# Order of x's load and h's transfers, place of h's transposes and sums, and slots of the second-level weight factors in a two-layer graph kernel

## The chip, the cores and the metric

The kernel runs on one core of a Trainium2 chip. The core has five engines with a program of their own each: TensorE (PE, matrix products), VectorE (DVE), ScalarE (ACT), GpSimd (POOL) and SyncE (SP, which here only starts transfers). The metric is device time in microseconds (us) of the whole program, median of several runs.

## What is computed

`x` is 64 x 256 x 512 in float32, `adj` a 256 x 256 matrix of zeros and ones. Cut to what matters:

```python
h = jnp.maximum(_layernorm(x, axis=-1), 0.0)
q, k, v = h @ Wq.T, h @ Wk.T, h @ Wv.T            # per batch, D = 512
rel = adjacency.T[None] * jnp.einsum('bnd,bmd->bnm', q, k)
rel = rel / jnp.linalg.norm(rel, axis=2, keepdims=True)
x = x + jnp.einsum('bnm,bmd->bnd', rel, v)        # layer 0
h = jnp.maximum(_layernorm(x, axis=-1), 0.0)
x = x + jnp.einsum('nm,bmd->bnd', adj, h) @ weight + bias   # layer 1
```

## The kernel before

**Tiles.** Batches go in 32 pairs of two. The x of a pair is a tile of 128 x 4 x 512 in one of five places of a ring (`x_ring`): pair i + 4 is loaded into the place that pair i - 1 leaves when its result has been stored. Wq and Wk are folded into one matrix M before the loop, so that the scores are h M h. Every large product is done by Strassen-Winograd's scheme with seven block products; the products with M (g), Wv (v) and the last weight (mix) take it a second level down for one part of the blocks. Such a scheme needs sums and differences of blocks made beforehand on DVE: `left_factors` (lines 173 to 176) for the moving side, `right_operands` (lines 135 to 138) for the other.

**Stages of one step.** `steady(i)` runs for i = 1 to 28 and works on five pairs at once: it applies the scores of pair i (`attend_and_v`, products of line 662, takes of line 669), makes the scores of pair i + 1 (`scores`, line 311), makes g and v of pair i + 2 (`g_and_v`, lines 287, 299, 478 and 525), turns h of pair i + 3, multiplies pair i by adj (`gather_steps`, line 739, copied out by ACT at line 743) and by the last weight (`mix_and_v`, lines 299 and 525, takes of lines 773 and 534). The first and last pairs have functions of their own.

**What sets the order.** PE, DVE and ACT run under a hand-written order: each stage is a list of products, and a dictionary says which small pieces of work are written down behind the product of that number ("slots"). An engine keeps that order: an instruction that waits holds up all that is behind it on its engine. SP and POOL are not in the hand-written order; their instructions follow a scheduler's order. On SP's queue, one step starts sixteen transfers of h (line 440), one load of x (line 90) and sixteen transfers of rel (line 586); POOL adds the bias in four instructions (line 723) and starts the store (line 794).

**h turned.** The normalised h of pair i + 3 must be transposed. Sixteen transfers move its 32 x 32 squares to their mirrored places (`place_blocks`, into the one tile `blocks`), and eight DVE instructions (`transpose_blocks`, line 450) turn each square. Then come the four sums of the left factors (lines 173 to 176, 128 x 512 each). The tile `blocks` is a scratch of ACT's row sums (lines 358 and 364) as well.

**v's differences.** `attend_operands` gives four steps `v_steps` (lines 135 to 138, into `v_room`, `v` and the two halves of `placed`), one for each of Winograd's right factors; the last is used by the last product of `attend_and_v` alone.

**A bank and its take.** A product goes to a bank of PSUM, and is then taken: the first into a block is copied by ACT (line 464 for g, 513 for v), the later ones are added by DVE (line 466 for g, 515 for v, 487 and 534 at the second level). A product that starts anew in `bank_a` has to wait for the take before it. In `g_and_v` the order of products is a1, c5, a6 with g1, v's a1, a7 with g2, v's c5, a4 with g3, numbered 0 to 6 for the slots.

Of the kernel before, what the change touches and what calls it, by code (L numbers as in the profile page):

```python
# [19 lines left out]
def kernel(  # L20
# [256 lines left out]
    def run_steps(steps, side):  # L277
        for at, step in enumerate(steps):
            step()
            run(side.get(at, ()))  # L280
# [153 lines left out]
    def place_blocks(i):  # L434

        h = H.pop(i)
        hv = h.rearrange("p c (d e) -> p c d e", e=P)
        for j in range(P // S):
            for k in range(P // S):
                nc.sync.dma_start(  # L440
                    out=blocks[ts(j, S), :, :, ts(k, S)], in_=hv[ts(k, S), :, :, ts(j, S)]
                )
# [275 lines left out]
    def add_bias(i):  # L718

        xt = flat(X[i])  # L720
        add = nc.gpsimd.tensor_tensor
        return [
            (lambda c=c: add(xt[:, c, :], xt[:, c, :], bias_bc, ALU.add)) for c in range(TC)  # L723
        ]
# [167 lines left out]
    w_right, w_steps = weight_operands(w_sb, "w")  # L892
    m_second, m_second_steps = second_right(m_right, "m2")
    wv_second, wv_second_steps = second_right(wv_right, "wv2")
    w_second, w_second_steps = second_right(w_right, "w2")
# [34 lines left out]
    def first_pairs(exact):  # L930


        sums = transposes_by_matmul(0)
        stats, root, end, relus = ln0(1)
        run(sums)
        project_g(0, {
            0: stats[0:1] + [lambda: load(3, nc.scalar)],
            1: stats[1:2] + [lambda: load(4, nc.scalar)],
            2: stats[2:4] + [root, load_w_and_bias], 3: [end] + relus,
            4: wv_steps[0:2], 5: wv_steps[2:3], 6: wv_steps[3:4],  # L940
        })
        place_blocks(1)
        turned1, sums1 = transpose_blocks(1)
        gs = g_operands(0)
        stats, root, end, relus = ln0(2)
        project_v(0, {
            0: gs[0:2], 1: gs[2:3] + stats[0:1], 2: gs[3:4] + stats[1:2], 3: stats[2:3],
            4: stats[3:4] + [root], 5: [end], 6: turned1[0:2],
        })
        masks, squares, norm_root, inverse, scales, place, turns = scores(0, {  # L950
            0: turned1[2:4], 1: turned1[4:6], 2: turned1[6:8], 3: relus[0:1] + sums1[0:1],
            4: relus[1:2] + sums1[1:2], 5: relus[2:3], 6: relus[3:4],
        })
        place_blocks(2)
        stats, root, end, relus = ln0(3)
        project_g(1, {
            0: sums1[2:4] + masks[0:1], 1: masks[1:2] + squares[0:2] + stats[0:1],
            2: squares[2:4] + stats[1:2], 3: [norm_root] + stats[2:3],
            4: [inverse] + scales + [place] + stats[3:4] + [root], 5: [end] + w_steps[0:1],
            6: w_steps[1:4],  # L960
        })
        gs = g_operands(1)
        turned2, sums2 = transpose_blocks(2)
        project_v(1, {
            0: gs[0:2], 1: gs[2:3] + turned2[0:2], 2: gs[3:4] + turned2[2:4] + relus[0:2],
            3: turned2[4:6] + relus[2:4] + w_second_steps[0:4],
            4: turned2[6:8] + m_second_steps[0:4],
            5: m_second_steps[4:8] + turns[0:2], 6: turns[2:4],
        })
        place_blocks(3)  # L970
        masks, squares, norm_root, inverse, scales, place, turns = scores(1, {
            0: sums2[0:1], 1: sums2[1:2], 2: sums2[2:3], 3: sums2[3:4], 5: w_second_steps[4:8],
        })
        stats, *parts = ln1(0, exact)
        h_second = second_h.pop(2)()
        attend(0, by_slot({c: [stats[c]] for c in range(TC)}, {
            0: masks[0:1], 1: masks[1:2] + squares[0:2], 2: squares[2:4] + [norm_root],
        }))
        turned3, sums3 = transpose_blocks(3)
        if exact:  # L980
            nc.vector.tensor_copy(adjt_r, adjt_sb)
        g, v = g_and_v(2, by_slot(layer_1(parts), {
            1: h_second + [inverse], 2: turned3[0:4], 3: scales + [place] + turned3[4:8],
            4: add_bias(0) + wv_second_steps[0:4], 5: sums3[0:2], 6: wv_second_steps[4:8],
        }))
        v_steps, rel_steps = attend_operands(1)
        y_products, y_steps = gather_steps(0, exact)
        run_steps(y_products, {
            0: sums3[2:3], 1: sums3[3:4], 2: y_steps[0:1], 3: v_steps[0:1],
        })  # L990
        y_second = second_of_y(0)
        totals, mean, row_squares, *norm0 = norm_by_scalar(flat(X[4]))
        run(y_steps[1:2])
        mixed = mix_and_v(0, g, v, {
            0: y_steps[2:4] + totals[0:2], 1: y_second[0:4] + totals[2:4],
            2: y_second[4:8] + [mean] + row_squares[0:2], 3: v_steps[1:2] + row_squares[2:4],
            4: turns + rel_steps[0:2] + norm0[0:2], 5: rel_steps[2:4] + v_steps[2:4],
        })
        return norm0[2], mixed, v

    def steady(i, exact, relu0, mixed, v):

        gs = g_operands(i + 1)
        relus0 = relus_of_h(i + 3, relu0)
        stats, root, end, relus, uppers, lowers = ln1(i, exact)
        halves = [stats[b * NC + t] for t in range(NC) for b in range(NB)]
        attend_and_v(i, mixed, v, {  # L1010
            0: relus0[0:2], 1: relus0[2:4] + gs[0:1], 2: gs[1:2],
            3: gs[2:3], 4: gs[3:4] + halves[0:1], 5: halves[1:2],
        })
        if i + 4 < NP:
            load(i + 4)
        place_blocks(i + 3)
        HL2.pop(i + 1)
        h_second = second_h.pop(i + 2)()
        masks, squares, norm_root, inverse, scales, place, turns = scores(i + 1, {
            0: halves[2:3], 1: halves[3:4] + h_second[0:1], 2: [root] + h_second[1:4],  # L1020
            3: [end] + relus[0:1], 4: relus[1:2],
        }, inside=True)
        turned, sums = transpose_blocks(i + 3)
        v_steps, rel_steps = attend_operands(i + 1)
        g, v = g_and_v(i + 2, {
            0: masks + squares + [norm_root] + turned[0:4] + [inverse] + scales + [place],
            1: uppers[0:2] + turned[4:8] + lowers[0:2],
            2: relus[2:4],
            3: uppers[2:4] + sums[0:2],
            4: lowers[2:3] + sums[2:4] + add_bias(i),  # L1030
            5: lowers[3:4] + v_steps[0:2],
        })
        y_products, y_steps = gather_steps(i, exact)
        run_steps(y_products, {2: y_steps[0:1], 3: turns})
        y_second = second_of_y(i)
        totals, row_squares, mean, root0, end0, relu0 = [], [], [], [], [], None
        if i + 4 < NP:
            totals, *middle, relu0 = norm_by_scalar(flat(X[i + 4]))
            mean, row_squares, root0, end0 = [middle[0]], middle[1], [middle[2]], [middle[3]]
        run(y_steps[1:2])  # L1040
        mixed = mix_and_v(i, g, v, {
            0: y_steps[2:4] + totals[0:2], 1: y_second[0:4] + totals[2:4],
            2: y_second[4:8] + mean + row_squares[0:2],
            3: rel_steps[0:2] + row_squares[2:4], 4: root0 + rel_steps[2:4] + end0,
            5: v_steps[2:4],
        })
        return relu0, mixed, v

    def last_pairs(exact, relu0, mixed, v):

        a, b, c = NP - 3, NP - 2, NP - 1
        gs = g_operands(b)
        stats, root, end, relus, uppers, lowers = ln1(a, exact)
        halves = [stats[e * NC + t] for t in range(NC) for e in range(NB)]
        attend_and_v(a, mixed, v, {
            1: gs[0:1], 2: gs[1:2], 3: gs[2:3], 4: gs[3:4] + halves[0:1], 5: halves[1:2],
        })
        h_second = second_h.pop(c)()
        masks, squares, norm_root, inverse, scales, place, turns = scores(b, {
            0: halves[2:3], 1: halves[3:4] + h_second[0:1], 2: [root] + h_second[1:4],  # L1060
            3: [end] + relus[0:1], 4: relus[1:2],
        }, inside=True)
        g, v = g_and_v(c, {
            0: masks + squares + [norm_root, inverse] + scales + [place],
            1: uppers[0:2] + lowers[0:2],
            2: relus[2:4],
            3: uppers[2:4],
            4: lowers[2:3] + add_bias(a),
            5: lowers[3:4],
        })  # L1070
        y_steps = gather(a, exact)
# [89 lines left out]
```

## Time and profile before

| | |
|---|---|
| median of 3 runs | 1763.59 us (1762.11 to 1766.94) |
| span of the profiled run | 1764.8 us, granted TensorE clock 0.998 |
| PE busy | 1707.8 us, 97% |
| DVE busy | 1535.3 us, 87% |
| ACT, POOL busy | 812.3 us, 225.2 us |
| one step of `steady` | 53.2 us where it is shortest, 53.9 us on average |

The last row is read from the starts of one product, g's a4, that occurs once a step: 165.47 us in the first step, 1621.61 us twenty-seven steps later, and 327.25 and 380.43 us for two that are close. A busy share of 97% does not say that 3% are to be had: the ends of matmuls are modelled in the profile, so that the share also hides short gaps. What counts is where a product starts later than the product before it would let it.

The views used are the list of waits (who waited for whom, in total, how often, the longest), the timeline (start, duration, engine, line, tiles, and in brackets the idle time before it and what ended it), the groups by line and shape, and the chain of work that ended last. Lines of the timeline that end in x4 are four instructions in a row, the duration being that of all.

### The profile page before, as it was taken

The page shows a single profiled execution, that of the slowest core. Times are in us where ns is not written, and L with a number is a line of the kernel's source. Part 1 is how long each engine was busy: PE and PEld are TensorE (multiplying, and loading weights), DVE is VectorE, ACT ScalarE, POOL GpSimd, SP SyncE. Part 2 cuts the span into 40 slices and gives each one's busy share as a digit, 9 for nine tenths or more (in the row PEclk, how much of TensorE's full clock was granted, in tenths as well). Part 3 has the DMA queues.
Part 4 walks back from the last instruction along what each step waited for, and adds up shares of the span by engine and source line. Part 5 has one row for each costly group of instructions (what it writes and reads, how often), then busy time and mean ns, then how long its engine had stood idle before and what let it go on. Part 6 is the DMA issues. An engine that isn't in the chain of part 4 may idle for free.

```text
span 1764.8 us, 28451 instructions
## 1 busy us (share of the span) xinstructions
PE 1707.8 (97%) x10274; PEld 1530.4 (87%) x10274; DVE 1535.3 (87%) x3336; ACT 812.3 (46%) x1835; POOL 225.2 (13%) x167
## 2 busy tenths in 40 slices
PE   9999999999999999999999999999999999999998
PEld 7878898888888888988888888889888888888986
DVE  6889899888898889898888988888988889889777
ACT  3444444544534544445544445444454444554331
POOL 0011100111101111001111001110011100111111
PEclk9999999999999999999999999999999999999999
DMA  7413333133332243332333322333224333233101
GB/s 236 65 23 84 80 76 70 30 82 85 77 78 44 55 85 83 74 76 46 59 84 78 78 47 51 84 80 76 59 38 84 84 74 75 47 58 60 34 19 59
DMA packets 425734, 122.56 MB, mean 69 GB/s; under 512 B 398064, under 2 KB 398832, under 8 KB 425584
## 3 DMA queue, kind: packets, MB, share of 16 engines
q1 hardware_dynamic: 412992, 80.28, 25.0%
q0 software_dynamic: 8432, 32.51, 5.3%
q10 hardware_dynamic: 4160, 7.87, 1.3%
q8 instruction: 83, 1.36, 0.3%
q14 instruction: 67, 0.55, 0.1%
HBM read 38.27 MB, written 33.55 MB: 41 GB/s over the span
## 4 chain that ended last, share of the span: by engine, by line
PE 41%; DVE 17%; issue 17%; SPq 14%; DMA 7%; ACT 4%; DVEq 0%; POOLq 0%; ACTq 0%
PE bank_a L299 14%; SPq L440 13%; PE py L739 5%; PE bank_a L287 4%; DMA out_dram<-x_ring 4%; DMA blocks<-h 3%; PE bank_e L525 3%; PE bank_c L299 3%; DVE ht L173 3%; PE bank_a L662 2%; ACT rel L579 2%; DVE ht L174 2%; PE bank_d L525 2%; DVE ht L450 2%; DVE h L711 2%
## 5 line engine op out<-in xcount | busy, mean ns | idle before, releaser
L723 POOL TENSOR_TENSOR x_ring<-x_ring,bias_bc 128x512 f32<-128x512 f32 x128 | 200.3, 1585 | 759.2 <-DVE rel L559 424.6
L287 PE MATMUL bank_a<-ht,m_t 128*128 128x256 f32 x768 | 188.5, 389 | 39.4 <-DVE g L466 24.1
L287 PEld LDWEIGHTS bank_a<-ht,m_t 128*128 128x128 f32 x768 | 142.3, 191 | 77.9 <-DVE g L466 35.3
L299 PE MATMUL bank_a<-wv_t,ht 128*128 128x256 f32 x768 | 181.8, 379 | 0.0
L299 PEld LDWEIGHTS bank_a<-wv_t,ht 128*128 128x128 f32 x768 | 143.4, 190 | 18.5 <-DVE v L515 0.2
L513 ACT COPY v<-bank_a 128x512 f32<-128x512 f32 x96 | 55.2, 575 | 215.2 <-PE bank_a L299 215.2
L364 ACT ACTIVATE blocks<-x_ring,sm 128x512 f32<-128x512 f32 x112 | 80.9, 722 | 123.8 <-DVE sm L361 122.0
L739 PE MATMUL py<-adjt_r,h 128*128 128x256 f32 x1024 | 126.5, 281 | 0.1
L711 DVE TENSOR_TENSOR h<-h2c,h 128x512 fp32r<-128x512 f32 x128 | 86.7, 698 | 43.4 <-ACT h L707 43.4
L342 ACT ACTIVATE h2c<-x_ring,nb,rs 128x512 f32<-128x512 f32 x128 | 97.5, 808 | 56.3 <-DVE nb L339 51.9
L299 PE MATMUL bank_a<-w_t,ys 128*128 128x256 f32 x512 | 121.4, 380 | 1.1 <-DVE x_ring L773 1.1
L794 POOL DMA_DIRECT2D out_dram<-x_ring x31 | 24.1, 776 | 759.2 <-issue 549.2
L739 PEld LDWEIGHTS py<-adjt_r,h 128*128 128x128 f32 x1024 | 120.6, 188 | 0.3 <-DVE h L711 0.3
L450 DVE STREAM_TRANSPOSE ht<-blocks 128x256 f32<-128x256 f32 x248 | 86.7, 409 | 39.2 <-DMA blocks<-h 36.4
L377 ACT ACTIVATE h<-x_ring,nb,rs 128x512 f32<-128x512 f32 x112 | 82.0, 802 | 65.9 <-PE bank_e L525 65.9
L299 PEld LDWEIGHTS bank_a<-w_t,ys 128*128 128x128 f32 x512 | 96.3, 190 | 15.4 <-DVE x_ring L773 1.9
L773 DVE TENSOR_TENSOR x_ring<-bank_a,x_ring 128x512 f32<-128x512 f32 x128 | 88.0, 687 | 23.7 <-PE bank_a L299 23.6
L743 ACT COPY yt<-py 128x512 f32<-128x512 f32 x128 | 75.1, 587 | 71.2 <-PE py L739 61.8
L311 PE MATMUL bank_a<-ht,gt 128*128 128x128 f32 x744 | 101.3, 279 | 1.1 <-DVE rel L559 1.1
L330 DVE BATCH_NORM_STATS2 st<-x_ring 128x6 f32<-128x512 f32 x144 | 97.8, 679 | 0.4
L464 ACT COPY g<-bank_a 128x512 f32<-128x512 f32 x96 | 56.0, 584 | 87.4 <-PE bank_a L287 87.4
L557 ACT COPY rel<-bank_a 128x256 f32<-128x256 f32 x96 | 35.8, 373 | 130.9 <-PE bank_a L311 91.3
(221 smaller groups left out, 4101.2 us busy)
## 6 DMA issues: line engine op xcount, KB each, us to landing
blocks<-h SPq DMA_DIRECT2D x496, 64.0 KB, 3.2
out_dram<-x_ring POOLq DMA_DIRECT2D x31, 1024.0 KB, 5.4
x_ring<-in_x_dram SPq DMA_DIRECT2D x28, 1024.0 KB, 6.0
placed<-rel SPq DMA_DIRECT2D x496, 32.0 KB, 2.0
x_ring<-in_x_dram ACTq DMA_DIRECT2D x4, 1024.0 KB, 5.5
wq_sb<-in_L_gnn_Wq_dram SPq DMA_DIRECT2D x4, 256.0 KB, 4.9
wk_sb<-in_L_gnn_Wk_dram ACTq DMA_DIRECT2D x4, 256.0 KB, 5.9
wv_sb<-in_L_gnn_Wv_dram ACTq DMA_DIRECT2D x1, 1024.0 KB, 5.4
```

Source lines behind the costliest of these rows:

```text
L287: nc.tensor.matmul(bank[:, e * HT_ : (e + 1) * HT_], right[n][:, d, ts(e, P)], left[n][:, d, :], start=(start and e == 0 and d == 0), stop ...
L299: nc.tensor.matmul(bank[:, b * HD : (b + 1) * HD], left[n][:, d, ts(b, P)], right[n][:, d, :], start=(start and b == 0 and d == 0), stop=( ...
L311: nc.tensor.matmul(bank[:, ts(b, P)], right[n][:, d, ts(b, P)], left[n][:, d, ts(b, P)], start=(start and b == 0 and d == 0), stop=(d == H ...
L330: nc.vector.bn_stats(st[:, c, :], src[:, c, :])
L342: nc.scalar.activation(dst, src[:, c, :], AF.Relu, bias=nb[:, c : c + 1], scale=rs[:, c : c + 1])
L440: nc.sync.dma_start(out=blocks[ts(j, S), :, :, ts(k, S)], in_=hv[ts(k, S), :, :, ts(j, S)])
L450: nc.vector.transpose(ht[:, d, half].rearrange("p (b n) -> p b n", b=NB), by_half[:, :, half, d])
L525: nc.tensor.matmul(out, left[k][n], right[k][n], start=start, stop=True, skip_group_check=True)
L711: nc.vector.tensor_sub(dst[:, 1, c, :], whole_h[c], dst[:, 0, c, :].bitcast(F32))
L723: (lambda c=c: add(xt[:, c, :], xt[:, c, :], bias_bc, ALU.add)) for c in range(TC)
L739: nc.tensor.matmul(pm[:, d, :], left[:, b * NC + m, ts(d0 + d, P)], right, start=(n == 0), stop=(n == len(terms) - 1),)
L773: nc.vector.tensor_add(xt[block], bank.rearrange("p (b e) -> p b e", b=NB), xt[block])
```

## The change

Five edits. In each step of `steady`, the sixteen transfers of h are put ahead of the load of x, the last four of h's transposes go from slot 1 of `g_and_v` to slot 3, and the four sums of h come behind all of the transposes, in slots 4 to 6. To make room for them, the four steps of v's differences each go one place later (the last of them into the next step's `attend_and_v`). In `first_pairs`, the second-level factors of Wv and of the last weight are made in other slots. No instruction is added or left out. The intent is that x's load, which must wait for a store, does not hold up the transfers of h, and that h's sums are not made before all its transposes.

```diff
@@ first_pairs
-            4: [inverse] + scales + [place] + stats[3:4] + [root], 5: [end] + w_steps[0:1],
-            6: w_steps[1:4],
+            4: [inverse] + scales + [place] + stats[3:4] + [root], 5: [end] + w_steps[0:2],
+            6: w_steps[2:4] + w_second_steps[0:4],
...
-            3: turned2[4:6] + relus[2:4] + w_second_steps[0:4],
+            3: turned2[4:6] + relus[2:4],
...
-            0: sums2[0:1], 1: sums2[1:2], 2: sums2[2:3], 3: sums2[3:4], 5: w_second_steps[4:8],
+            0: sums2[0:1], 1: sums2[1:2], 2: sums2[2:3], 3: sums2[3:4], 4: w_second_steps[4:8],
...
-            4: add_bias(0) + wv_second_steps[0:4], 5: sums3[0:2], 6: wv_second_steps[4:8],
+            4: add_bias(0), 5: sums3[0:2],
...
-            0: sums3[2:3], 1: sums3[3:4], 2: y_steps[0:1], 3: v_steps[0:1],
+            0: wv_second_steps[0:4], 1: wv_second_steps[4:8], 2: y_steps[0:1], 3: v_steps[0:1],
...
-            4: turns + rel_steps[0:2] + norm0[0:2], 5: rel_steps[2:4] + v_steps[2:4],
+            4: turns + rel_steps[0:2] + norm0[0:2], 5: rel_steps[2:4] + v_steps[2:3] + sums3[2:4],
         })
-        return norm0[2], mixed, v
+        return norm0[2], v_steps[3:4], mixed, v
@@ steady
         attend_and_v(i, mixed, v, {
-            0: relus0[0:2], 1: relus0[2:4] + gs[0:1], 2: gs[1:2],
+            0: relus0[0:2] + v_last, 1: relus0[2:4] + gs[0:1], 2: gs[1:2],
             3: gs[2:3], 4: gs[3:4] + halves[0:1], 5: halves[1:2],
         })
+        place_blocks(i + 3)
         if i + 4 < NP:
             load(i + 4)
-        place_blocks(i + 3)
...
             0: masks + squares + [norm_root] + turned[0:4] + [inverse] + scales + [place],
-            1: uppers[0:2] + turned[4:8] + lowers[0:2],
+            1: uppers[0:2] + lowers[0:2],
             2: relus[2:4],
-            3: uppers[2:4] + sums[0:2],
-            4: lowers[2:3] + sums[2:4] + add_bias(i),
-            5: lowers[3:4] + v_steps[0:2],
+            3: uppers[2:4] + turned[4:8],
+            4: lowers[2:3] + sums[0:1] + add_bias(i),
+            5: lowers[3:4] + sums[1:3], 6: sums[3:4] + v_steps[0:1],
         })
...
-        run_steps(y_products, {2: y_steps[0:1], 3: turns})
+        run_steps(y_products, {0: v_steps[1:2], 2: y_steps[0:1], 3: turns})
...
-            5: v_steps[2:4],
+            5: v_steps[2:3],
         })
-        return relu0, mixed, v
+        return relu0, v_steps[3:4], mixed, v
@@ last_pairs
         attend_and_v(a, mixed, v, {
-            1: gs[0:1], 2: gs[1:2], 3: gs[2:3], 4: gs[3:4] + halves[0:1], 5: halves[1:2],
+            0: v_last, 1: gs[0:1], 2: gs[1:2], 3: gs[2:3], 4: gs[3:4] + halves[0:1],
+            5: halves[1:2],
         })
```

More of the change, by code (lines that the diff above doesn't have):

```diff
@@ L996, in first_pairs, with steady @@
             2: y_second[4:8] + [mean] + row_squares[0:2], 3: v_steps[1:2] + row_squares[2:4],
-            4: turns + rel_steps[0:2] + norm0[0:2], 5: rel_steps[2:4] + v_steps[2:4],
+            4: turns + rel_steps[0:2] + norm0[0:2], 5: rel_steps[2:4] + v_steps[2:3] + sums3[2:4],
         })
-        return norm0[2], mixed, v
-    def steady(i, exact, relu0, mixed, v):
+        return norm0[2], v_steps[3:4], mixed, v
+    def steady(i, exact, relu0, v_last, mixed, v):
         gs = g_operands(i + 1)
@@ L1044, in steady, with last_pairs @@
             3: rel_steps[0:2] + row_squares[2:4], 4: root0 + rel_steps[2:4] + end0,
-            5: v_steps[2:4],
+            5: v_steps[2:3],
         })
-        return relu0, mixed, v
-    def last_pairs(exact, relu0, mixed, v):
+        return relu0, v_steps[3:4], mixed, v
+    def last_pairs(exact, relu0, v_last, mixed, v):
         a, b, c = NP - 3, NP - 2, NP - 1
```

## The prediction

> **What bounds the kernel now.** I began with the engine shares: PE is busy for 1707.8 of 1764.8 us, so it sets the time, and only what makes PE start late can be won. So the second view is the list of waits, for PE, then for DVE and for the queue of SP. Columns: engine, line, "<-" the one waited for, us in total, times, longest.
>
> ```profile
> PE bank_a L287 <- DVE g L466: 24.1, 28, 0.9
> PE bank_a L287 <- ACT g L464: 15.2, 21, 2.0
> ...
> DVE ht L450 <- DMA blocks<-h: 36.4, 26, 2.8
> ...
> SPq L90 <- DMA out_dram<-x_ring: 64.4, 27, 3.7
> ```
>
> Two waits, both in g_and_v and both about once a step, make up nearly all of PE's waiting inside the loop. The first one, in the timeline of PE and of DVE around 750 us (start, us, engine, line):
>
> ```profile
> 752.88 1.89 PE L299 MATMUL bank_c<-wvt_sb,ht 128*128 128x256 f32 x8
> 755.66 1.99 PE L287 MATMUL bank_a<-ht,m_t 128*128 128x256 f32 x8 [0.88 <-DVE g L466]
> ...
> 751.02 1.70 DVE L173 TENSOR_TENSOR ht<-ht 128x512 f32<-128x512 f32 x1
> 752.76 1.65 DVE L174 TENSOR_TENSOR ht<-ht 128x512 f32<-128x512 f32 x1
> 754.33 0.68 DVE L466 TENSOR_TENSOR g<-bank_c,g 128x512 f32<-128x512 f32 x1
> 754.93 0.68 DVE L466 TENSOR_TENSOR g<-bank_a,g 128x512 f32<-128x512 f32 x1
> ...
> 750.90 2.95 POOL L723 TENSOR_TENSOR x_ring<-x_ring,bias_bc 128x512 f32<-128x512 f32 x2 [5.60 <-ACT h2c L342]
> ```
>
> Eight such products follow each other in 1.73 us where nothing waits (744.07 to 745.79), so a4 could start at 752.88 + 1.73 = 754.61; it starts at 755.66. The wait costs 1.05 us, 0.17 more than its bracket says, since the modelled end of a matmul lies late. It waits for the take of a7, which stands on DVE behind two sums of h that last 1.70 and 1.65 us, although the same form elsewhere takes 0.68 (line 175 on ht, 679 ns on average). POOL's bias additions run at just that time.
>
> The second wait, by the queue of SP:
>
> ```profile
> 779.87 2.88 SPq L440 DMA_DIRECT2D blocks<-h  x3
> 785.21 0.37 SPq L90 DMA_DIRECT2D x_ring<-in_x_dram  x1
> 785.62 10.58 SPq L440 DMA_DIRECT2D blocks<-h  x13
> ```
>
> The scheduler put x's load behind three transfers of h; it waits for the store, and the other thirteen wait with it from 782.75 to 785.21. The chain of waits goes on from here: landing, four transposes (line 450), the reciprocal of the norms (line 576), ACT's four scalings (line 579), and behind these ACT's copy of a6 (line 464), for which a7 waits. In the step at 964 us the last of h issues at 959.39 and lands at 961.48, and a7 starts at 966.83, 1.78 us after its time of 963.32 + 1.73; near 755 us the transfers are quicker and a7 does not wait.
>
> Check by the length of a step: the shortest is 53.2 us with the first wait alone, so 53.2 - 1.05 = 52.15 us without waits. From 165.47 to 1621.61 us there are 27 steps, 1456.1 us; 27 x 52.15 = 1408.1. So **48 us** are lost, which agrees with 24.1 + 15.2 us and 0.17 for each of 49 waits (47.6).
>
> **What the Trainium skill says.** "SBUF — State Buffer", in "SBUF: two separate sides", says that DVE and GpSimd share a pair of ports under an exclusive lock, which a DVE operation with two inputs in SBUF needs for its whole time. The trace agrees: the sums of h (two inputs in SBUF) take 1.70 us beside POOL instead of 0.68, while eight transposes (one input) from 104.70 us take 2.72 us beside it, 0.34 each as anywhere, and L466, with one input in PSUM, 0.65. "DMA: Bandwidth & Descriptors", in "Anatomy of one DMA — SWDGE (gpsimd) path", says that a wait on a semaphore happens on the issuing sequencer before dispatch; that is the held queue of SP above.
>
> **The change part by part**, in the step from 742 us, in the old clock.
>
> *Load behind h.* h is normalised from 776.9 us on, as now, and its transfers issue from 779.87 without the pause. The three beside the store took 0.96 each (2.88), undisturbed ones 0.68. Six at 0.96 until the store ends near 785.2, then ten at 0.68: the last starts near 792, and with 2.1 to 3 us of landing all is there at 794 to 795 instead of 798.2. DVE needs it when the second mask is done, 797.4 now, 796.2 once PE loses no time. Bounds: 0.68 for all gives 792.2, 0.96 for all 779.87 + 15 x 0.96 + 3 = 797.3. I take 794.5. The load issues near 792.7 instead of 785.2 and takes 6 us; its first reader is ACT's row sum at 762.7 + 53 = 816, so that is free. The transfers of rel start at 801 behind it. What is won: DVE's 36.4 us, and so PE's second wait whole, 15.2 + 21 x 0.17 = 18.8 us. Norms, scalings and copies then come 0.3 us earlier than in the step shown, since the transposes start at 744.1, not 744.9.
>
> *Transposes 4 to 7 into slot 3, sums to slots 4 to 6.* Now DVE runs four transposes (1.35 us) and then `lowers`, for which it waits 1.45 us; afterwards it waits about 2.8 us there, which costs nothing, as g1's takes stand behind `lowers` in both orders. Worked down DVE's order with the start-to-start times of the trace (0.60 for 512 elements, 0.34 for 256 or a transpose, 0.12 more behind its own input): lowers at 748.8 and 749.4, g1's takes at 750.0 and 750.35, transposes 750.7 to 752.0, takes of c5 and a7 at 752.0 and 752.65, a7's product being done near 752.1. a4's bank is free at 753.3, before 754.61: PE's first wait goes, 1.05 us a step. POOL's second pair now ends by 753.5 and meets transposes and takes from PSUM. Behind that: g2's take 753.3, lowers and the first three sums to 756.8, g3's takes at 757.0 and 757.45, the last sum 758.05, v_steps at 758.65 and 759.4, and y's first sum at 760.0. That needs ACT's second copy of y, which comes at 761.0 - 1.05 = 759.95. So DVE is just in time, with nothing to spare. Behind it stand rel's four transposes (line 589; rel lands near 760) and L174 of y, for which mix's c5 waits; that chain has 0.1 us of room now, and keeps it if DVE is not late. For a lateness I allow 0.1 us a step, 3 us; the bound is 0.7 us, all of a displaced operation.
>
> *v_steps one place later.* The fourth (0.69 us, line 138) leaves the place ahead of the take of `one` (line 669 at 778.15), so the take comes 0.6 us earlier. `six` starts at 778.88, while its bank's sequence would let it at 778.24 + 0.44 = 778.69: 0.19 us a step more, 28 x 0.19 = 5 us. In its new place it delays no take: `five` is taken near 779.0 (779.08 now). The factor is used by the last product only.
>
> *First pairs.* Eight small differences of Wv leave slots 4 and 6 and stand among y's products instead of two sums; mix's c5, late by 1.12 us at 118.02, should be on time. The two sums come ahead of the take at 134.99, with one v_step gone: 0.7 us more on the wait of 0.85. a4's wait (0.64) stays. Net -0.5 us. The factors of the last weight only move between slots where PE shows no wait: DVE's time there lies beside PE. `last_pairs`: v_last moves as above; a4's wait at 1621.61 (0.73) stays, since POOL and lowers there are untouched.
>
> Sum: 48 us less the last pair's 0.9, plus 0.9 of the first step (165.47), 48; plus 5 and 0.5, less 3 of lateness: 50.5. 1763.6 - 50.5 = 1713.
>
> **The rivals.** *A new wait at y's sums*: DVE's crowd before 760 us makes L174 late, by 0.4 to 0.7 us a step. For it: no room in my table, and the wait exists already in the first pairs (1.12 us). Against: DVE loses 2 us of lock time a step. 27 x 0.65 = 17 us given back: 1731. *h still late*: sharing with the store slows h to the upper bound (797.3, or more) and the second wait stays: 48 - 18.8 = 29 us won, with the rest about 1733. For it: transfers are near full beside the store. Against: beside the load, which moved as much, thirteen took 10.6 to 12.8 us. *Slower*: h and the store delay each other, and h lands 2.4 us later than now (16 at 0.96 with the 5.4 us of landing seen beside the store: 779.87 + 15.4 + 5.4 = 800.6 against 798.2). Then 27 x 2.4 = 65 us more less 28: near 1800.
>
> **How the numbers follow.** Likeliest case 0.72, 1713, with 1707 to 1722 inside it (no lateness and all small waits gone; lateness 0.4). New wait at y 0.15, h still late 0.08, slower 0.03, nothing moved 0.02. The range reaches over most of the first two cases: 1706 to 1732. Faster 0.95, same 0.02, slower 0.03.
>
> **What would show it.** Right: PE's waits of line 287 for g (L466, L464) shrink to single ones in first and last pairs; DVE's wait for h's landing under 5 us; the sums of h at 0.7 us, so DVE busy falls by 29 x 2 = 57 us to about 1478; DVE's wait at line 711 grows to about 80 us; a step lasts 52.0 to 52.3 us; SP starts sixteen transfers of h in a row, then the load. Wrong: a wait of PE in mix for `yt` in every step, sums still above 1.5 us, h landing after the masks, or a granted clock below 0.998 once PE has no pauses.

## Result, and the profile after

The changed kernel takes **1708.45 us** (median, 1707.91 to 1709.14), the kernel before 1765.26 us in the same session: a ratio of 0.968 (95% interval 0.966 to 0.970), 57 us less. The forecast was 1713 us, 1706 to 1732; the result lies near its fast end.

Shares of the page, the kernel after:

```profile
PE 1686.4 (99%) x10274; PEld 1530.5 (90%) x10274; DVE 1479.2 (87%) x3336; ACT 812.0 (48%) x1835; POOL 213.0 (12%) x167
...
PE 89%; DVE 5%; SPq 2%; ACT 1%; DMA 1%; issue 1%; DVEq 0%; ACTq 0%
```

The second line is the chain of work that ended last: 89% of it is PE now, where PE was 41% before and DVE, SP's queue and transfers made up much of the rest. DVE does the same 3336 instructions in 56 us less. The list of waits, kernel after, for PE and DVE:

```profile
PE bank_c L299 <- DVE yt L174: 2.0, 5, 0.7
...
PE bank_a L287 <- DVE g L466: 0.6, 1, 0.6
...
DVE h L711 <- ACT h L707: 80.0, 29, 2.8
...
DVE ht L450 <- DMA blocks<-h: 1.4, 1, 1.4
```

The two waits of g are gone but for one in the first pairs (0.6 us); the wait for ACT's copy of a6 is not listed at all. DVE's largest wait in total, at line 711, has grown from 43.4 to 80.0 us; no wait of PE in the list goes back to that line. The timeline of one step, kernel after:

```profile
782.75 1.89 PE L299 MATMUL bank_c<-wvt_sb,ht 128*128 128x256 f32 x8
784.48 1.89 PE L287 MATMUL bank_a<-ht,m_t 128*128 128x256 f32 x8
...
780.73 1.41 DVE L450 STREAM_TRANSPOSE ht<-blocks 128x256 f32<-128x256 f32 x4
782.07 0.65 DVE L466 TENSOR_TENSOR g<-bank_c,g 128x512 f32<-128x512 f32 x1
782.64 0.67 DVE L466 TENSOR_TENSOR g<-bank_a,g 128x512 f32<-128x512 f32 x1
...
784.16 0.68 DVE L173 TENSOR_TENSOR ht<-ht 128x512 f32<-128x512 f32 x1
...
780.62 2.51 POOL L723 TENSOR_TENSOR x_ring<-x_ring,bias_bc 128x512 f32<-128x512 f32 x2 [5.31 <-ACT h2c L342]
...
756.91 12.35 SPq L440 DMA_DIRECT2D blocks<-h  x16
769.42 0.50 SPq L90 DMA_DIRECT2D x_ring<-in_x_dram  x1
```

a4 starts 1.73 us after v's c5, at once. Beside POOL's second pair of additions (780.62 to 783.13) there are transposes and takes from PSUM now, none of them slower than elsewhere, and the first sum of h comes at 784.16 with 0.68 us. POOL gains too: that pair takes 2.51 us, and took 2.95 beside the sums. SP starts all of h in a row.

### The profile page after: what moved, and what is told of

Same layout as the page of the kernel before. It is cut to its first block, busy times and chain, and to the rows that moved or that the text cites. A ratio compares the mean times of both kernels' runs of the same rounds, so it can differ in the third digit from the quotient of the medians.

```text
span 1706.3 us, 28450 instructions
## 1 busy us (share of the span) xinstructions
PE 1686.4 (99%) x10274; PEld 1530.5 (90%) x10274; DVE 1479.2 (87%) x3336; ACT 812.0 (48%) x1835; POOL 213.0 (12%) x167
## 4 chain that ended last, share of the span: by engine, by line
PE 89%; DVE 5%; SPq 2%; ACT 1%; DMA 1%; issue 1%; DVEq 0%; ACTq 0%
PE bank_a L299 24%; PE bank_a L287 11%; PE bank_a L311 7%; PE bank_a L662 6%; PE bank_e L525 6%; PE bank_c L299 6%; PE py L739 6%; PE bank_d L525 5%; PE bank_c L311 3%; PE bank_c L287 3%; PE bank_c L662 3%; PE bank_e L478 3%; SPq L586 2%; PE bank_d L478 2%; PE bank_b L311 2%; PE bank_b L662 1%
## 5 line engine op out<-in xcount | busy, mean ns | idle before, releaser
L723 POOL TENSOR_TENSOR x_ring<-x_ring,bias_bc 128x512 f32<-128x512 f32 x128 | 188.2, 1491 | 745.1 <-DVE rel L559 437.1
L287 PE MATMUL bank_a<-ht,m_t 128*128 128x256 f32 x768 | 181.5, 379 | 0.6 <-DVE g L466 0.6
L287 PEld LDWEIGHTS bank_a<-ht,m_t 128*128 128x128 f32 x768 | 145.8, 190 | 20.8 <-DVE g L466 1.0
L311 PEld LDWEIGHTS bank_a<-ht,gt 128*128 128x128 f32 x744 | 90.4, 192 | 3.6 <-DVE rel L559 0.6
```

The costliest lines, as they stand in the source:

```text
L287: nc.tensor.matmul(bank[:, e * HT_ : (e + 1) * HT_], right[n][:, d, ts(e, P)], left[n][:, d, :], start=(start and e == 0 and d == 0), stop ...
L311: nc.tensor.matmul(bank[:, ts(b, P)], right[n][:, d, ts(b, P)], left[n][:, d, ts(b, P)], start=(start and b == 0 and d == 0), stop=(d == H ...
```

## Experiments

Each is set beside the kernel before, measured again with it: 1765.8 us with the first four, 1768.7 with the next three and the first run of the last, 1766.6 with the two runs that close the section. The theory: two causes, each with its own wait of PE. SP's queue is held by x's load, so that a7 waits for ACT's copy of a6; and h's sums are slow beside GpSimd's additions (the shared port of the prediction), so that a4 waits for the take of a7. The first rival puts all of it on the earlier landing of h, the second says that the new order of transposes makes the landing harmless.

**x's load ahead again, in the changed kernel**

```diff
-        place_blocks(i + 3)
         if i + 4 < NP:
             load(i + 4)
+        place_blocks(i + 3)
```

> The changed kernel with the load of x ahead of h's transfers again, all else as changed. Theory of two causes (held queue and shared port, each with its own wait of PE): the wait of g's a7 for ACT's copy of a6 comes back, 15.2 us as listed before plus 0.27 us for each of 21 (0.17 that the list leaves out and 0.10 for the first matmul after a pause), 21 us: about 1729 us; g's a4 does not wait, as its take moves with the rest. Rival 1 (all of the gain is the earlier landing of h; the sums only mattered because DVE was late): about 1765 us, a4 waits again. Rival 2 (the new place of transposes and sums makes the landing harmless): 1708 us, no change against the changed kernel.

Measured: 1716.4 us (ratio to before 0.972, 0.971 to 0.974), **8 us** more than the changed kernel, not 21. Its waits:

```profile
PE bank_a L287 <- ACT g L464: 4.7, 8, 1.6
...
SPq L90 <- DMA out_dram<-x_ring: 17.3, 27, 4.6
```

The wait for ACT's copy is back, as the theory had it, and a4 does not wait in the loop: both rivals fall. But it is 4.7 us and not 15.2, because SP waits for the store for 17.3 us in all, where the kernel before waits 64.4. So something else in the change made the store end earlier. The experiment below that moves the last of v's differences alone looks for it. y's sum (line 174) is also late a little more often, 3.5 us in 7 steps where the changed kernel has 2.0 in 5.

**x's load behind, in the kernel before**

> The kernel before with one edit, x's load behind h's transfers. Two causes: the wait for ACT's copy of a6 goes (21 us), and DVE's order in g_and_v comes about 0.3 us earlier, since the first transposes no longer wait, so the wait of a4 for the take of a7 shrinks from 0.88 to some 0.55 us but stays in all 28 steps (9 us): about 1735 us. Rival 1 (all is the landing of h): about 1709 us, a4 does not wait. Rival 2 (landing harmless): 1765 us.

The edit is the one above turned round. Measured: 1740.6 us (0.986, 0.984 to 0.987), **25 us** less than before.

```profile
PE bank_a L287 <- DVE g L466: 21.1, 29, 0.7
...
DVE ht L450 <- DMA blocks<-h: 0.7, 1, 0.7
```

DVE waits for the landing of h in one step only, PE's wait for ACT's copy is gone, and a4 still waits in every step, mostly by 0.73 us instead of 0.88. The starts of the products, summed over the 27 steps from the first a4 of `steady` to the last, show where the gain lies: 23.1 us at a7 (its wait, and its own length) and 2.9 at a4, 26.0 in all. Of the 23.1 us, 1.5 are one a7 (1184.47) that took longer in the trace of the kernel before, in a stretch with a granted clock of 0.59; they are no gain of the edit. I had expected the a4 wait to shrink by twice as much; POOL's additions start 0.28 us earlier too, counted from g's a1, and the sums stay beside them (1.71 us).

**Half of the bias left out, in the kernel before**

```diff
-            (lambda c=c: add(xt[:, c, :], xt[:, c, :], bias_bc, ALU.add)) for c in range(TC)
+            (lambda c=c: add(xt[:, c, :], xt[:, c, :], bias_bc, ALU.add)) for c in range(2)
```

> The kernel before with the bias added to pieces 0 and 1 of each pair only; the additions to pieces 2 and 3 are left out, which are the ones that run on GpSimd beside the first two sums of h. Order of DVE, PE and ACT as before. Shared port: the two sums take 0.68 us each instead of 1.70 and 1.65, the take of a7 is done before a4's turn, and 28 x 1.15 = 32 us go: about 1733 us, the wait for ACT's copy of a6 stays. Rival (the two sums stand ahead of the takes and their number is what costs, or something else slows them): the sums keep 1.65 us or more, the time stays at 1765 us.

This kernel leaves out half of the bias. Measured: 1737.3 us (0.983, 0.981 to 0.985), **28 us** less. Of this kernel, a line of the groups by shape (busy us, mean ns, idle before and its reason):

```profile
L173 DVE TENSOR_TENSOR ht<-ht 128x512 f32<-128x512 f32 x32 | 21.8, 680 | 0.4 <-ACT ht L431 0.4
```

and its timeline of DVE in one step:

```profile
742.96 0.68 DVE L173 TENSOR_TENSOR ht<-ht 128x512 f32<-128x512 f32 x1
743.67 0.69 DVE L174 TENSOR_TENSOR ht<-ht 128x512 f32<-128x512 f32 x1
744.28 0.68 DVE L466 TENSOR_TENSOR g<-bank_c,g 128x512 f32<-128x512 f32 x1
744.88 0.68 DVE L466 TENSOR_TENSOR g<-bank_a,g 128x512 f32<-128x512 f32 x1
```

The sums stand ahead of the takes as before, yet the first takes 680 ns on average instead of 1578, and a4 waits no more in the loop. So it was not their number but GpSimd's work beside them. That this is a lock on a port is the prediction's reading; the runs show the durations. The same slowing is still to be seen in the changed kernel: beside POOL's first pair of additions, line 562 on `rel`, with two inputs in SBUF, takes 1.23 us at 772.93 and 0.68 at 771.80. The 4 us that are missing are a wait for y's sum (line 174, 5.3 us in 9 places; 1.1 us in one place before, in the first pairs).

**The last of v's differences back ahead of `one`'s take, in the changed kernel**

```diff
-            5: v_steps[2:3],
+            5: v_steps[2:4],
         })
-        return relu0, v_steps[3:4], mixed, v
+        return relu0, v_steps[4:4], mixed, v
```

> The changed kernel with the last of v's differences back in slot 5 of the mix, ahead of the take of `one`. If that displaced operation is what made `six` start late before: 0.19 us and 0.10 for the restart come back in 28 steps, 8 us, about 1716 us, and `six` starts 0.64 us after the second level product before it began instead of 0.45. Rival (the step is only moved, and PE has slack there): 1708 us.

Measured: 1719.2 us (0.974, 0.972 to 0.975), **11 us** more than the changed kernel. In this kernel, and then in the changed one, `six` and the product before it:

```profile
762.41 0.61 PE L525 MATMUL bank_d<-wvt_sb,hs 128*128 128x128 f32 x4
763.04 1.13 PE L662 MATMUL bank_a<-placed,rel 128*128 128x256 f32 x4
```

```profile
807.02 0.61 PE L525 MATMUL bank_d<-wvt_sb,hs 128*128 128x128 f32 x4
807.47 1.03 PE L662 MATMUL bank_a<-placed,rel 128*128 128x256 f32 x4
```

`six` starts 0.63 us after that product, where it is 0.45 in the changed kernel. The shortest step grows from 51.73 to 52.01 us: 0.28, of which 0.19 is the late start itself and 0.10 that `six` takes longer to the next product (0.97 us instead of 0.87). The remaining 3 us are waits for y's sum, 4.0 us in 8 steps instead of 2.0 in 5.

**The slots of the first pairs as before, in the changed kernel**

> The changed kernel with the slots of first_pairs as before (all of it, the last of v's differences of pair 1 too). If the first pairs are worth what their two waits say: mix's c5 waits about 1.1 us for y's sum again, the wait of 1.45 us in pair 0's attention falls back to 0.85: within 1 us of the changed kernel's 1708.5. Rival (part of the 57 us is won in the first pairs): some 5 us slower or more.

The edit takes `first_pairs` from the kernel before, with nothing handed on to the first step. Measured: 1711.1 us (0.968, 0.966 to 0.970), a ratio that can't be told from the changed kernel's 0.968. In the trace the way from the first pairs' a4 to the next is 55.93 us, with the new slots 55.32: 0.6 us, the half microsecond foreseen.

**Transposes and sums of h alone, in the kernel before**

```diff
-            1: uppers[0:2] + turned[4:8] + lowers[0:2],
+            1: uppers[0:2] + lowers[0:2],
             2: relus[2:4],
-            3: uppers[2:4] + sums[0:2],
-            4: lowers[2:3] + sums[2:4] + add_bias(i),
-            5: lowers[3:4] + v_steps[0:2],
+            3: uppers[2:4] + turned[4:8],
+            4: lowers[2:3] + sums[0:2] + add_bias(i),
+            5: lowers[3:4] + sums[2:4] + v_steps[0:2],
```

> The kernel before with the last four transposes of h moved to slot 3 and the four sums to slots 4 and 5, everything else in place (load ahead, v's differences in their old slots). If moving the two-input sums off GpSimd's time is all that the sums' edit does: the wait of a4 goes, 28 x 1.15 = 32 us, about 1734 us, and the two sums take 0.68 us. The wait for ACT's copy of a6 stays near 15 us. Rival (without the moved v's differences DVE is too late for y): a new wait of c5 for y's sum (line 174) of 0.3 us or more in every step, 1743 us or more.

Measured: 1742.5 us (0.985, 0.983 to 0.988), **26 us** less than the kernel before beside it.

```profile
PE bank_a L287 <- ACT g L464: 15.6, 21, 2.0
PE bank_c L299 <- DVE yt L174: 4.9, 8, 1.3
```

In the loop a4 waits no more, and the wait for ACT's copy has stayed, as foreseen: two causes apart. The time lies between theory (about 1734) and rival (1743 or more), close to the rival: y's sum is listed as late in 7 of the steps and once in the first pairs, not in all.

**The last of v's differences moved alone, in the kernel before**

```diff
-            0: relus0[0:2], 1: relus0[2:4] + gs[0:1], 2: gs[1:2],
+            0: relus0[0:2] + v_last, 1: relus0[2:4] + gs[0:1], 2: gs[1:2],
...
-            5: v_steps[2:4],
+            5: v_steps[2:3],
```

> The kernel before with one edit: the last of v's differences goes behind the first take of the next step's attention. Direct effect: `six` is on time, 28 x 0.29 = 8 us. If this edit also lets the store of the pair before start earlier (DVE's last take of the mix stands right behind that operation), SyncE's wait for the store falls from 64 to about 20 us, h lands over 1 us earlier, and the wait of a7 for ACT's copy falls from 15.2 to about 5 us, 10 to 13 us more: 1745 us. Rival (no such coupling): 1757 us, and SyncE's wait stays at 64 us.

Measured: 1742.5 us (0.985, 0.982 to 0.987), **26 us** less, for one operation in another place. Its waits, and then its timeline of SP's queue:

```profile
PE bank_a L287 <- ACT g L464: 6.2, 10, 1.6
...
SPq L90 <- DMA out_dram<-x_ring: 15.4, 27, 2.1
```

```profile
772.07 3.56 SPq L440 DMA_DIRECT2D blocks<-h  x3
776.11 0.37 SPq L90 DMA_DIRECT2D x_ring<-in_x_dram  x1
```

The start of the store, in the kernel before and then in this one:

```profile
779.71 0.77 POOL L794 DMA_DIRECT2D out_dram<-x_ring  x1 [25.85 <-issue]
```

```profile
771.18 0.77 POOL L794 DMA_DIRECT2D out_dram<-x_ring  x1 [25.17 <-issue]
```

The coupling is there. DVE's last take of the mix (line 534, the last that writes to the pair that is stored) stands behind that operation. The profile names no releaser of the store, but in every kernel here it starts 0.96 us (median) after that take does. With the operation gone from its place, POOL starts the store at 771.18, 0.89 us ahead of h's first transfer; in the kernel before it is 0.16 us (779.71 and 779.87). The store then lands in 4.8 us instead of 5.4 (medians), and x's load issues 4.04 us after h's first transfer instead of 5.34. So the rest of h is queued 1.3 us earlier although it still stands behind the load. Summed over the 27 steps, 13.3 us are won at a7, 8.0 at `six` and 0.6 at a4, 21.8 in all. The kernel before ran 2 to 3 us slower beside these experiments than beside the others, so 26 is rather too much.

**Two transposes of rel behind y's sum, in the changed kernel**

```diff
-        run_steps(y_products, {0: v_steps[1:2], 2: y_steps[0:1], 3: turns})
+        run_steps(y_products, {0: v_steps[1:2], 2: y_steps[0:1], 3: turns[0:2]})
...
-        run(y_steps[1:2])
+        run(y_steps[1:2] + turns[2:4])
```

> The changed kernel, but in each step two of the four transposes of rel stand behind the sum of y for which the mix's c5 waits (line 174), not ahead of it. If that sum is now what PE is late for: c5 starts 0.10 us earlier in each step and a6 0.07, and the few waits of 0.2 to 0.7 us listed for it go, 3 to 5 us: about 1704.5 us. Rival (PE's start there is set by something else, or the takes that come later make it up): 1708.5 us or slower.

Measured: **1704.5 us** (0.964, 0.962 to 0.966). A second run set it beside the changed kernel.

> The changed kernel again, beside the one with rel's transposes split, on the same chip. 1706 to 1712 us.

> The kernel with rel's four transposes split around y's sum, again, beside the changed kernel. If the two small waits behind y's sums (0.17 us a step and the listed ones) are really won: 4 to 5 us below the changed kernel in the same call. If the difference seen so far came from the chip: equal within 2 us.

The changed kernel: 1708.5 us (1707.7 to 1711.8); with the split: 1704.1 us (1703.5 to 1705.1). The difference of 4.3 us is real, and this is the fastest kernel of all. What is won is seen in PE's timeline at the mix's first two products, in the changed kernel:

```profile
739.01 1.89 PE L299 MATMUL bank_a<-w_sb,yt 128*128 128x256 f32 x8
740.84 1.96 PE L299 MATMUL bank_c<-w_sb,yt 128*128 128x256 f32 x8
```

and in the kernel with the split (its first run):

```profile
738.45 1.89 PE L299 MATMUL bank_a<-w_sb,yt 128*128 128x256 f32 x8
740.17 1.89 PE L299 MATMUL bank_c<-w_sb,yt 128*128 128x256 f32 x8
```

1.83 us from one to the other in the first, 1.72 in the second: in most steps a tenth of a microsecond that no bracket shows, since the modelled end hides it. Summed over the 27 steps, c5 starts 4.4 us earlier and a6 another 1.6, and the product behind a6 gives 1.7 back.

## Why the prediction was right, and where it was off

**What bounds the kernel, and the two waits: right.** The a4 wait comes from GpSimd's additions beside h's sums, shown from both sides: by leaving out GpSimd's work in the old order, and by the new order with GpSimd's work in place. The wait for ACT's copy is the held queue: putting the load behind removes it alone.

**The load behind h: right.** Sixteen transfers issue in 12.7 us (median of 28 steps; 12.35 in the one shown), where I had 12.6 with six slowed, and all of h is there 14.4 us after its first transfer, where I had 14.6. DVE's wait for h fell from 36.4 to 1.4 us. The rival with h landing too late did not come. That the times fit so well is in part luck: with the load behind h and the store in its old place (x's load behind, in the kernel before) they are 13.4 and 15.2 us, and the earlier store, which I did not foresee, makes up for it. Even so DVE waits for h in one step only.

**DVE's order worked down: right to a tenth.** Counted from the start of g's a1 (742.34 in the step of the prediction, 772.33 in the step shown above), the take of a7 was put at 10.31 us and came at 10.31; `lowers` at 6.46 and came at 6.52 (778.85). DVE busy was to be 1478 us and is 1479.2.

**The rival with y's sum: partly there.** I allowed 3 us of lateness, 0.1 us a step. The starts of the mix's c5 and a6 come 4.6 us later in the 27 steps than in the kernel before, and the split experiment gets 4.3 us back: five waits of up to 0.7 us, and 0.1 us in most other steps. That does not come near the 17 us of the rival.

**Terms that were mis-sized.** The forecast had 50.5 us. The medians differ by 57, the two profiled spans by 58.5: 27 steps are 56.0 us shorter (53.93 against 51.86 on average, where I had named 52.0 to 52.3), the way from the first pairs to the loop 1.5, and what lies ahead of it 1.05.

Part of it is what follows a4. The product behind it, before (a4 at 755.66) and after (a4 at 784.48):

```profile
757.49 0.61 PE L478 MATMUL bank_e<-hs,m_t 128*128 128x128 f32 x4
```

```profile
786.21 0.61 PE L478 MATMUL bank_e<-hs,m_t 128*128 128x128 f32 x4
```

For the 27 steps the forecast comes to 49.4 us (48.1 less 0.9 and 2.9, plus 27 x 0.19). The 6.6 us between come from four terms, which give about 7:

- *What a pause costs.* I priced a wait at its bracket plus 0.17. The product behind a pause is longer itself: from a4 to the next product it is 1.83 us in the kernel before (755.66 to 757.49), 1.73 after (784.48 to 786.21). Summed over the 27 steps, a4 is 2.7 us shorter now and `six` 2.7: 5.4 us that I left out, most of the difference. a7 is 4.1 us shorter as well, but the 48 us came from the length of steps and had that in them. (1.5 of the 4.1 is the single slow product at 1184.47.)
- *The step without waits.* I took 53.2 us for the shortest step. The last of the 27 (1568.66 to 1621.61) lasts 52.95, and less its wait of 0.73 + 0.17 that is 52.05 instead of 52.15: up to 2.7 us more were to be had. That the list of waits gave 47.6 beside the 48 was in part luck. It counts two waits that lie outside the 27 steps (0.64 at 108.64 and 0.73 at 165.47) and leaves out the longer a7.
- *The wait at 1621.61.* I read it as the last pairs' and left it standing. It is the twenty-eighth step's and went with the rest, 0.9 us. The last pairs have no such wait in either kernel.
- *Lateness at the mix,* 4.6 us instead of 2.9, goes the other way.

The displaced operation ahead of `one`'s take was sized rightly, 5.2 us for its late start where I had 5. The 1.05 us ahead of the loop, for which I had nothing, are not shown to come from the change: the kernel with rel's transposes split has the same first pairs as the changed one, yet its first pairs' a4 starts at 108.53 us, where it is 107.59 in the changed kernel and 108.64 in the kernel before.

**A cause that I didn't see.** The last of v's differences also held back the store. In the changed kernel the earlier store brings nothing, because h no longer waits for it: with the difference put back there, a step grows by 0.28 us, all of it `six`. But it is the main reason why undoing the load alone costs 8 us and not 21: the moved difference alone wins 13.3 of the 23.1 us at a7. The load alone, the sums alone and the moved difference alone give 25, 26 and 26 us, 77 in all, and the change gives 57. In the 27 steps of the traces they are 26.0, 24.3 and 21.8 us against 56.0, and the overlap can be read there: some 13 us at a7 and 3 at a4 are won by more than one of the three.

## What to carry to other kernels

When an engine is 97% busy, compare start to start with the same product elsewhere: a bracket of 0.9 us was a loss of 1.15. On an engine whose order is fixed, look at what runs on GpSimd at the same moment before counting operations. Here transposes and takes from PSUM were no slower beside its additions, and sums with two inputs in SBUF took 1.5 to 1.6 us on average instead of 0.68, so the first belong there and the second elsewhere. On a queue, put what waits for a store behind what is ready, and ask of each operation ahead of a last take which store it holds back.

## What was not expected of the hardware

A product of eight matmuls that starts after a pause takes 0.10 us more than one that follows another (1.83 against 1.73 us), and `six`, with four, as much more (0.97 against 0.87); why, no run here shows. And when a large store starts, relative to many small transfers, matters to the store itself: started 0.88 us ahead of h's transfers it landed in 4.8 us in the median of each of seven profiles, started 0.16 us ahead in 5.4 us in each of five.
